# The tail of a convolution–attention–state-space kernel: frequencies in another order, most of the second piece read inside the loop

## The chip, the cores and the metric

The kernel runs on one core of one Trainium2 chip. The metric is device time in microseconds (us) of one execution. A core has a matrix engine (TensorE, PE in the profile, its weight loads PEld), a vector engine (VectorE, DVE), a scalar engine (ScalarE, ACT), GpSimd (POOL) and a sequencer that issues transfers (SyncE, SP). Sixteen DMA engines move data between DRAM and the on-chip memory (SBUF, 128 partitions); transfers are issued here from SP's and from ACT's queue. Each queue issues in order, and an issue that waits holds up everything behind it on its queue.

## The reference, cut to what matters

The input is 8 images of 32 x 32 positions with 128 channels, float32. Layer 0 is a group norm and an attention; layer 1 is a bidirectional state-space block and then a spectral filter bank, and every block adds its input back. The change touches only the end of the last one, which is, for every batch `b`, position `t` and output channel `e`:

```
U_plus  = causal convolution of u with K=16 filters over t          (by FFT)
U_minus = the same of u * (-1)^t, times (-1)^t
out     = einsum('btkd,k,kde->bte', U_plus,  sigma**0.25, M_plus)
        + einsum('btkd,k,kde->bte', U_minus, sigma**0.25, M_minus)
        + sum over i<3 of u[t-i] @ M_u[i]
t       = t + out * keep          # keep: the weight of the bank that a hard softmax picks
```

The kernel does the convolutions with a transform of its own: 128 odd frequencies per block, products with a matrix per frequency, and the transform back.

## The kernel before, in words

**The frequency loop.** The spectra of all batches lie in DRAM (`ud`). A *chunk* is `FC` = 8 of the `NF` = 128 frequencies, so there are 16 chunks. In pass `c` of the loop (`for c in range(-1, chunks)`, L1840) TensorE builds the matrices of chunk `c+1` (`matrices`, L1594, copied out by DVE and ACT at L1605 and L1607) and multiplies the spectra of chunk `c` with the matrices of chunk `c` (`apply`, L1751). A pass has four steps `n`; steps 0 and 1 make the chunk's first four frequencies, steps 2 and 3 its last four. `gather` (L1767 to L1773) adds up the products into `sums`, and `store` (L1779) writes the sums of four frequencies to DRAM, `yd[frequency, block, batch, 2, 4, channel]`, 256 KB. A frequency's row of `yd` has 64 KB: two blocks of 512 positions, each with eight batches; a quarter of it (one block, four batches) is 16 KB and contiguous.

**The pieces.** After the loop the sums are transformed back in four *pieces*, `(k, h)`: block `k`, batches `4h` to `4h+3`. A piece is a tile `yt` of 128 partitions, one frequency in each, 16 KB per partition. For each piece DVE makes `z` (four operations, L1879), TensorE multiplies `inv` with `yt` and `z` for four values of `r` (L1889), DVE multiplies with `keep` and adds the residual, which lies in DRAM as `xa` (L1896), and ACT's queue stores the result (L1899). The last piece is done in two halves of two batches. All of TensorE, DVE, ACT, POOL and SP run in the order in which the program is written (`tc.manual_schedule(engines=ALL_IN_ORDER)`).

**How the pieces get in.** In the order of SP's queue:

- In each pass, the row of the first piece for the eight frequencies of the chunk before is read back from `yd` into `early_yt`, eight rows of 16 KB to eight neighbouring partitions (`fetch`, L1788). SP's transfers of a pass are tied to a product of TensorE (`behind`), which places them within the pass. In the last pass a second fetch reads four more rows, as soon as their store has landed.
- In the last pass the first residual is loaded, 1 MB (`load_residuals`, L1805).
- After the loop the last four frequencies of the first piece are moved from `sums` in SBUF to `early_yt` (`move`, four transfers of 16 KB, L1799), and the last `store` is issued.
- Then come the second piece (`load_piece`, L1864: 112 rows on SP, which need only stores that have long landed, and 16 rows on ACT, which need the last store), its residual, the third piece with its residual and the fourth piece with its residual. A piece is 2.1 MB, a residual 1.05 MB. From the third piece on, the loads read all 128 rows and so wait for the last store.

The pieces 2 to 4 and a residual lie in the room of a chunk's matrices that is no longer needed (`room`).

**The order of the frequencies.** `odd` (L326) holds for each frequency its number 2f+1; the tables of the transform there (`fwd`) and of the filters (`taps`) are made from it, and `alt` (L393) holds the sign (-1)^f. The table of the transform back (`inv`) is made from the partition's number, so partition p of a piece must hold frequency p. Before the change the f-th row of `yd` is frequency f.

Of the kernel before, what the change touches and what calls it, by code (L numbers as in the profile page):

```python
# [14 lines left out]
P = 128  # L15
B = 8
# [16 lines left out]
FC = 8  # L33
PI_1024 = 0.0030679615757712823
# [11 lines left out]
def fast_kernel(ctx: ExitStack, tc: tile.TileContext, a: dict, out: bass.AP, bad: bass.AP):  # L46
# [273 lines left out]
    def transforms(pool, tables):  # L320


        def over_2048(t):
            nc.vector.tensor_scalar(t, t, 1.0 / 2048.0, None, ALU.mult)

        odd = counted(pool, [2, NF], [[512, 2], [2, NF]], 1, 0, "odd")  # L326
        place = counted(pool, [4], [[1, 4]], 0, 4, "place")
        over_2048(place)
        by_place = [(fwd[:, k : k + 1], odd[:, 0:1, :], place[:, k : k + 1]) for k in range(4)]
        turns(by_place[:2])  # L330
        yield
        odd_row = counted(pool, [1], [[1, 1]], 1, 2, "odd_row")
        places = counted(pool, [4, P], [[1, 4], [4, P]], 0, 0, "places")
        over_2048(odd_row)
        yield
        turns(by_place[2:])
        yield
        for _ in angles(pool, fwd, "fwd"):
            yield
        yield  # L340
        turns([(inv, places, odd_row[:, 0:1])])
        for _ in angles(pool, inv, "inv"):
            yield
        yield
        lag = counted(pool, [2, 2], [[-256, 2], [1, 2]], 510, -2, "lag")
        over_2048(lag)
        for h in range(2):
            for r in range(2):
                t = pool.tile([P, 2, 2, NF], F32, name=f"lags{h}_{r}")
                turns([(t, odd, lag[:, h, r : r + 1])])  # L350
                for _ in angles(pool, t, f"lags{h}_{r}"):
                    pass
                tables.append(t)
                yield
        for t in tables:
            sines(t)

    def transform_taps(pool, ps, tables):
# [34 lines left out]
        alt = pool.tile([P, NF // 2, 2], F32, name="alt")  # L393
        nc.gpsimd.memset(alt, 1.0)
        nc.gpsimd.memset(alt[:, :, 1], -1.0)
        alt = alt.rearrange("p f i -> p (f i)")
# [1155 lines left out]
    with ExitStack() as s:  # L1552
# [170 lines left out]
        with ExitStack() as s2:  # L1723
# [60 lines left out]

            def fetch(c, n, rows, other):

                at = slice(c * FC + n * 4, c * FC + n * 4 + rows)
                t = nc.sync.dma_start(  # L1788
                    early_yt[at].rearrange("p b i q e -> p (b i) (q e)"),
                    yd[at, 0, 0:4].rearrange("f b i q e -> f (b i) (q e)"),  # L1790
                )
                behind(t, other)

            def move(c, n, yt, piece):

                at = c * FC + n * 4
                for f in range(4):
                    rows = stored[c, n][f * 32 + piece * 8 : f * 32 + piece * 8 + 8]
                    nc.sync.dma_start(  # L1799
                        yt[at + f : at + f + 1].rearrange("p b i q e -> p (b i) (q e)"),  # L1800
                        rows.rearrange("x q e -> x (q e)"),
                    )

            def load_residuals(k, b, n, other=None):
                t = nc.sync.dma_start(  # L1805
                    res[k][:, b : b + n].rearrange("p b r c -> p b (r c)"),
                    xa[b : b + n, :, k].rearrange("b p r c -> p b (r c)"),
                )
                behind(t, other)

            def amid_products(c, n, made):

                last = c + 1 == chunks
                if n == 0 and c > 0:
                    store(c - 1, 1, made)
                if n == 3 and c > 0:
# [3 lines left out]
                if last and n == 3:  # L1820
                    fetch(c, 0, 4, made)
                if last and n == 0:
                    load_residuals(1, 0, 4, made)
                if not last and n in (1, 2):
# [6 lines left out]
            for c in range(-1, chunks):  # L1831
# [4 lines left out]
                else:  # L1836

                    room = chunk_matrices(c + 1, first_gs)
                    res = [room[:, :32, :], mp.tile([P, 32, C], F32, tag="mst", name="res1")]
                    res = [t.rearrange("p (b r) c -> p b r c", b=B) for t in res]  # L1840
# [13 lines left out]
            pieces = [(k, h) for k in range(NB) for h in range(2)]  # L1854
            yts = [early_yt]
            for n in range(1, 4):
                yts.append(room[:, 32 * n : 32 * n + 32].rearrange("p (b i q) c -> p b i q c", i=2, b=4))
            move(chunks - 1, 1, yts[0], 0)
            store(chunks - 1, 1, None, nc.sync)

            def load_piece(n, rows, engine):

                k, h = pieces[n]
                engine.dma_start(  # L1864
                    yts[n][rows].rearrange("p b i q c -> p (b i) (q c)"),
                    yd[rows, k, h * 4 : h * 4 + 4].rearrange("f b i q e -> f (b i) (q e)"),
                )

            load_piece(1, slice(0, NF - 2 * FC), nc.sync)
            load_piece(1, slice(NF - 2 * FC, NF), nc.scalar)  # L1870
            load_residuals(1, 4, 4)
            for n in range(2, 4):
                load_piece(n, slice(0, NF), nc.sync)
                load_residuals(0, 4 * n - 8, 4)
            for yt, (k, h) in zip(yts, pieces):
# [6 lines left out]
                size = 2 if (k, h) == pieces[-1] else 4  # L1882
                for b in range(0, 4, size):
                    bs = slice(b, b + size)
                    to = res[blk][:, h * 4 + b : h * 4 + b + size]
# [18 lines left out]
                    )  # L1904

# [805 lines left out]
```

## Time and profile before

| | us |
|---|---|
| median of 3 runs | 1382.64 (1382.20 to 1387.87) |
| the profiled execution | 1384.28 |
| its span, first to last instruction | 1382.6 |
| one pass of the loop, 1304.00 to 1320.60 | 16.60 |
| last product of the loop (L1751) ends | 1332.7 |
| first matmul of the pieces 1, 2, 3, 4 (L1889) | 1338.50, 1349.18, 1358.16, 1368.80 |
| stores of the result issued (L1899) | 1348.05, 1357.11, 1367.81, 1374.93, 1376.53 |

All times within the execution are counted from the span's start. Besides the page, which sums up an execution, the trace answers for a stretch how long each engine was busy in it, what granted clock TensorE had, which share of the time the 16 DMA engines were busy and how many GB/s they moved. A timeline lists instructions in order of time: start, duration, engine, line, operation, `written<-read`, count, and in brackets how long the engine had been idle and what ended that. `SPq` and `ACTq` are the issues of transfers; the transfer itself goes on after them. The trace also has each packet that a DMA engine moved, with its size and duration, and the times at which a transfer's semaphore was raised, once by each DMA engine that took part: the last of these is its landing.

### The profile page before, as it was taken

To read this page: it belongs to the slowest core of one execution; us is meant where nothing else is said; L and a number is where in the kernel's file an instruction comes from. 1 tells how busy PE (TensorE), PEld (TensorE's weight loads), DVE (VectorE), ACT (ScalarE), POOL (GpSimd) and SP (SyncE) were. 2 spreads that over 40 slices of the span, in tenths; PEclk is the share of its full clock that TensorE was granted. 3 is DMA by queue.
4 is the path that set the end of the run, shared out by engine and by line. 5 is a ranking of instruction groups with operands and counts; after the bars stand their busy time and mean duration, and the time that the engine had idled before them with its cause. 6 is when DMAs were issued, how large, how long until landed. Compare 5 with 4: busy or idle time off the path is not lost. (4 is left out here: it accounts for less than half of the span.)

```text
span 1382.6 us, 47750 instructions
## 1 busy us (share of the span) xinstructions
PE 1323.1 (96%) x20926; PEld 838.4 (61%) x20926; DVE 1102.9 (80%) x2144; ACT 922.9 (67%) x1429; POOL 551.9 (40%) x606
## 2 busy tenths in 40 slices
PE   7999999999999899999999999998999999999976
PEld 4333333333333566666666666665899999999953
DVE  5789889788868688988898989899775777777744
ACT  5766676766757788888888888787554655555510
POOL 3411986875920333435343434343693211111100
PEclk9999999999999999999999999999999999999999
DMA  7200111111000533434444544441388122222258
GB/s 175 55 2 2 35 44 40 46 48 39 24 9 2 128 87 78 109 78 109 93 94 93 117 94 112 93 110 33 93 275 258 51 78 76 75 77 75 73 156 331
DMA packets 139881, 123.26 MB, mean 89 GB/s; under 512 B 45268, under 2 KB 122708, under 8 KB 135060
## 3 DMA queue, kind: packets, MB, share of 16 engines
q1 hardware_dynamic: 137504, 115.67, 32.3%
q10 hardware_dynamic: 2160, 4.46, 0.9%
q8 instruction: 166, 2.72, 0.8%
q14 instruction: 51, 0.42, 0.1%
HBM read 78.09 MB, written 34.08 MB: 81 GB/s over the span
## 5 line engine op out<-in xcount | busy, mean ns | idle before, releaser
L809 ACT ACTIVATE pr<-pt 128x1024 f32<-128x1024 f32 x256 | 248.1, 1021 | 105.0 <-PE pt L804 104.0
L834 DVE TENSOR_TENSOR two<-pr,pr 128x1024 f32<-128x1024 f32 x128 | 165.0, 1329 | 15.1 <-ACT pr L809 15.1
L1607 ACT COPY gs<-pg 128x512 f32<-128x512 f32 x256 | 132.6, 601 | 60.8 <-PE pg L1594 60.3
L1605 DVE COPY gs<-pg 128x512 f32<-128x512 f32 x256 | 158.9, 684 | 12.7 <-PE pg L1594 9.5
L804 PE MATMUL pt<-q,k 32*128 32x512 f32 x1024 | 162.4, 651 | 6.1 <-ACT pr L809 4.2
L1594 PE MATMUL pg<-taps,mst 32*128 32x128 f32 x4096 | 146.6, 279 | 1.8 <-DVE gs L1605 1.1
L1594 PEld LDWEIGHTS pg<-taps,mst 32*128 32x128 f32 x4096 | 133.2, 186 | 15.2 <-issue 12.1
L825 PE MATMUL po<-pr,v 128*32 128x512 f32 x1024 | 140.6, 610 | 0.0
L1751 PE MATMUL pg<-gs,u 128*32 128x128 f32 (+1 forms) x4096 | 128.5, 277 | 2.4 <-issue 2.4
L1030 POOL TENSOR_TENSOR ec<-ec,ct 128x2048 f32<-128x2048 f32 x16 | 83.7, 5230 | 112.4 <-ACT ct L1110 57.1
L1072 DVE SCALAR_TENSOR_TENSOR xs<-xp,cw,xs 128x1024 f32<-128x1024 f32 x96 | 122.5, 1283 | 2.2 <-issue 0.2
L1582 POOL TENSOR_SCALAR u<-u 128x128 f32<-128x128 f32 x64 | 34.1, 533 | 217.7 <-DMA u<-ud 197.4
L1751 PEld LDWEIGHTS pg<-gs,u 128*32 128x32 f32 (+1 forms) x4096 | 112.2, 141 | 10.1 <-issue 2.6
L1094 PE MATMUL pb<-bxt,wbc 128*128 128x512 f32 x256 | 114.0, 597 | 3.6 <-ACT zs L1085 3.6
L804 PEld LDWEIGHTS pt<-q,k 32*128 32x128 f32 x1024 | 49.6, 186 | 88.9 <-ACT pr L809 27.1
L1302 POOL TENSOR_TENSOR rms<-rms_v,mhalf 128x8 f32<-128x8 f32 x16 | 26.6, 1660 | 157.2 <-DVE rms_v L1300 157.2
L1193 DVE SCALAR_TENSOR_TENSOR state<-state,dec,pst 128x64 f32<-128x64 f32 x448 | 87.3, 275 | 1.1
L1094 PEld LDWEIGHTS pb<-bxt,wbc 128*128 128x128 f32 x256 | 47.1, 189 | 60.4 <-issue 55.0
L825 PEld LDWEIGHTS po<-pr,v 128*32 128x32 f32 x1024 | 27.8, 110 | 89.7 <-issue 86.4
L1016 POOL TENSOR_TENSOR lm<-cs,lm 128x2048 f32<-128x2048 f32 x16 | 57.9, 3622 | 58.0 <-DVE xs L1072 34.7
L845 PE MATMUL pd<-two,ones 128*32 128x512 f32 x512 | 74.2, 618 | 2.4 <-DVE two L834 2.2
L1026 ACT ACTIVATE lm<-lm 128x1024 f32<-128x1024 f32 x64 | 65.7, 1052 | 6.8 <-POOL lm L1016 6.6
(312 smaller groups left out, 2787.7 us busy)
## 6 DMA issues: line engine op xcount, KB each, us to landing
lm<-cd SPq DMA_DIRECT2D x32, 512.0 KB
ec<-cd SPq DMA_DIRECT2D x32, 512.0 KB
ud<-sp SPq DMA_DIRECT2D x8, 1024.0 KB
u<-ud SPq DMA_DIRECT2D x64, 128.0 KB
yd<-sums SPq DMA_DIRECT2D x32, 256.0 KB
moved<-state SPq DMA_DIRECT2D x48, 128.0 KB
X<-in_x SPq DMA_DIRECT2D x8, 512.0 KB
part_p<-in_L_ffn_M_phi_plus SPq DMA_DIRECT2D x32, 128.0 KB
```

What stands on the lines that cost most here:

```text
L804: nc.tensor.matmul(pt[:, i, :], lhsT=k[rows, j * P : (j + 1) * P], rhs=q[rows, cols], start=True, stop=True)
L809: nc.scalar.activation(pr[:, 2 * g : 2 * g + 2, :].rearrange("p i t -> p (i t)"), pt.rearrange("p i t -> p (i t)"), AF.Exp, scale=SCALE,)
L825: nc.tensor.matmul(po[rows, :], lhsT=vs[b][:, j, rows], rhs=pr[:, h, :], start=(j == 0), stop=(j == NT - 1))
L834: nc.vector.tensor_tensor(two, sums["pr"][:, 2 * g : 2 * g + 2, :], pr[:, 2 * g : 2 * g + 2, :], ALU.add)
L1030: t = nc.gpsimd.tensor_tensor(u.ec, u.ec, u.ct.unsqueeze(1).to_broadcast([P, NH, NT, L]), ALU.mult)
L1072: u.convolved = nc.vector.scalar_tensor_tensor(acc, xp[:, at : at + T], cw[u.d][:, n, i : i + 1], acc, ALU.mult, ALU.add)
L1094: nc.tensor.matmul(u.pb[:, i * 512 : (i + 1) * 512], lhsT=wbc[u.d][:, k, :], rhs=xt[:, at : at + 512], start=(k == 0), stop=(k == KC - 1),)
L1193: nc.vector.scalar_tensor_tensor(u.state[:, k, h, :], u.state[:, k - 1, h, :], u.dec[:, c, h, j : j + 1], u.pst[c][:, j, h, :], ALU.mult, ...
L1594: nc.tensor.matmul(pts[g][:, e, :], lhsT=mst[rows, n * 4 + e, :], rhs=taps[rows, cols].rearrange("p f q m i -> p (f q m i)"), start=True, ...
L1605: nc.vector.tensor_copy(to, frm)
L1607: nc.scalar.copy(to, frm)
L1751: product = nc.tensor.matmul(py[t * 32 : t * 32 + 32 - 16 * m, q // 2, :], lhsT=u[:, i, m:, :, :, q * FC + f].rearrange("p k b i -> p (k b ...
```

## The change

1. **Order of frequencies.** Row `j*16+e` of `yd` (e = 0 to 15, j = 0 to 7) now holds frequency `e*8+j`: `odd` and `alt` are made in that order. `inv` is as it was, so that row belongs to partition `e*8+j`. The 16 rows of a pair of chunks `j` go to 16 partitions that lie 8 apart; `places` gives that slice of partitions.
2. **Early rows.** `fetch` and `move` write to those partitions. All four moves are on SP, as before.
3. **First residual.** It has a tile of its own (`first_res`) and is loaded in eight parts of 128 KB, one in each of the passes 2 to 9, behind the first store of the pass.
4. **Second piece.** In the last pass seven pairs (`load_rows`, 16 rows, 256 KB each) are read in the loop: two in step 0, two in step 1, one in step 2, two in step 3, the last two ahead of the four-row fetch. After the loop one pair is left, which holds the last chunks and so waits for the last store. The load on ACT's queue is gone.
5. **Third and fourth piece.** They are still one transfer each on SP, to 128 partitions in order, but the source is read as `(j e) -> e j`: 16 rows 64 KB apart on the outside, 8 steps of 1 MB within.
6. **Residuals.** One tile per piece instead of one per block; the sizes and their places in the order of SP after the loop are as before.
7. **Last piece.** It is done in parts of 2, 1 and 1 batches instead of 2 and 2.

```diff
+FR = 16
...
-        odd = counted(pool, [2, NF], [[512, 2], [2, NF]], 1, 0, "odd")
+        odd = counted(pool, [2, NF // FR, FR], [[512, 2], [2, NF // FR], [2 * NF // FR, FR]], 1, 0, "odd")
+        odd = odd.rearrange("p i j e -> p i (j e)")
...
-        alt = pool.tile([P, NF // 2, 2], F32, name="alt")
+        alt = pool.tile([P, NF // FR // 2, 2, FR], F32, name="alt")
         nc.gpsimd.memset(alt, 1.0)
         nc.gpsimd.memset(alt[:, :, 1], -1.0)
-        alt = alt.rearrange("p f i -> p (f i)")
+        alt = alt.rearrange("p j i e -> p (j i e)")
...
+            def places(row, n):
+
+                j, e = divmod(row, FR)
+                at = e * (NF // FR) + j
+                return slice(at, at + (n - 1) * (NF // FR) + 1, NF // FR)
+
             def fetch(c, n, rows, other):
 
-                at = slice(c * FC + n * 4, c * FC + n * 4 + rows)
+                at = c * FC + n * 4
                 t = nc.sync.dma_start(
-                    early_yt[at].rearrange("p b i q e -> p (b i) (q e)"),
-                    yd[at, 0, 0:4].rearrange("f b i q e -> f (b i) (q e)"),
+                    early_yt[places(at, rows)].rearrange("p b i q e -> p (b i) (q e)"),
+                    yd[at : at + rows, 0, 0:4].rearrange("f b i q e -> f (b i) (q e)"),
                 )
                 behind(t, other)
...
+            pieces = [(k, h) for k in range(NB) for h in range(2)]
+            first_res = yp.tile([P, 4, 4, C], F32, name="first_res")
+            res, yts = [first_res], [early_yt]
...
+            def load_first_residual(part, other):
+
+                b, h = divmod(part, 2)
+                t = nc.sync.dma_start(
+                    first_res[:, b, 2 * h : 2 * h + 2].rearrange("p r c -> p (r c)"),
+                    xa[b, :, NB - 1, 2 * h : 2 * h + 2].rearrange("p r c -> p (r c)"),
+                )
+                behind(t, other)
+
+            def load_rows(n, j, other=None):
+
+                k, h = pieces[n]
+                t = nc.sync.dma_start(
+                    yts[n][places(j * FR, FR)].rearrange("p b i q c -> p (b i) (q c)"),
+                    yd[j * FR : (j + 1) * FR, k, h * 4 : h * 4 + 4].rearrange("f b i q e -> f (b i) (q e)"),
+                )
+                behind(t, other)
+
+            def load_piece(n):
+
+                k, h = pieces[n]
+                nc.sync.dma_start(
+                    yts[n].rearrange("p b i q c -> p (b i) (q c)"),
+                    yd[:, k, h * 4 : h * 4 + 4].rearrange("(j e) b i q c -> e j (b i) (q c)", e=FR),
+                )
 
             def amid_products(c, n, made):
 
                 last = c + 1 == chunks
                 if n == 0 and c > 0:
                     store(c - 1, 1, made)
+                    if 2 <= c < 10:
+                        load_first_residual(c - 2, made)
                 if n == 3 and c > 0:
                     fetch(c - 1, 0, FC, made)
                 if n == (2 if last else 3):
                     store(c, 0, made)
-                if last and n == 3:
-                    fetch(c, 0, 4, made)
-                if last and n == 0:
-                    load_residuals(1, 0, 4, made)
-                if not last and n in (1, 2):
+                if last:
+                    for j in ((0, 1), (2, 3), (4,), (5, 6))[n]:
+                        load_rows(1, j, made)
+                    if n == 3:
+                        fetch(c, 0, 4, made)
+                elif n in (1, 2):
                     for part in (2 * n - 2, 2 * n - 1):
                         load_part(us[c + 1], c + 1, part, made)
...
-            move(chunks - 1, 1, yts[0], 0)
+            move(chunks - 1, 1, 0, nc.sync)
+            move(chunks - 1, 1, 1, nc.sync)
+            move(chunks - 1, 1, 2, nc.sync)
+            move(chunks - 1, 1, 3, nc.sync)
             store(chunks - 1, 1, None, nc.sync)
...
-            load_piece(1, slice(0, NF - 2 * FC), nc.sync)
-            load_piece(1, slice(NF - 2 * FC, NF), nc.scalar)
-            load_residuals(1, 4, 4)
+            load_rows(1, NF // FR - 1)
+            load_residuals(1)
             for n in range(2, 4):
-                load_piece(n, slice(0, NF), nc.sync)
-                load_residuals(0, 4 * n - 8, 4)
+                load_piece(n)
+                load_residuals(n)
...
-                size = 2 if (k, h) == pieces[-1] else 4
-                for b in range(0, 4, size):
+                b = 0
+                for size in (2, 1, 1) if (k, h) == pieces[-1] else (4,):
...
+                    b += size
```

More of the change, by code (lines that the diff above doesn't have):

```diff
@@ L1791, in fetch, with move @@
                 )
                 behind(t, other)
[L1794 to L1804, printed above, removed]
+            def move(c, n, f, engine):
+                rows = stored[c, n][f * 32 : f * 32 + 8]
+                engine.dma_start(
+                    early_yt[places(c * FC + n * 4 + f, 1)].rearrange("p b i q e -> p (b i) (q e)"),
+                    rows.rearrange("x q e -> x (q e)"),
+                )
@@ L1805, in load_residuals @@
+            pieces = [(k, h) for k in range(NB) for h in range(2)]
+            first_res = yp.tile([P, 4, 4, C], F32, name="first_res")
+            res, yts = [first_res], [early_yt]
+            def load_residuals(n, other=None):
+                k, h = pieces[n]
                 t = nc.sync.dma_start(
-                    res[k][:, b : b + n].rearrange("p b r c -> p b (r c)"),
-                    xa[b : b + n, :, k].rearrange("b p r c -> p b (r c)"),
+                    res[n].rearrange("p b r c -> p b (r c)"),
+                    xa[4 * h : 4 * h + 4, :, NB - 1 - k].rearrange("b p r c -> p b (r c)"),
@@ L1811, in amid_products @@
+            def load_piece(n):
+                k, h = pieces[n]
+                nc.sync.dma_start(
+                    yts[n].rearrange("p b i q c -> p (b i) (q c)"),
+                    yd[:, k, h * 4 : h * 4 + 4].rearrange("(j e) b i q c -> e j (b i) (q c)", e=FR),
+                )
             def amid_products(c, n, made):
@@ L1838, in fast_kernel @@
                     room = chunk_matrices(c + 1, first_gs)
-                    res = [room[:, :32, :], mp.tile([P, 32, C], F32, tag="mst", name="res1")]
-                    res = [t.rearrange("p (b r) c -> p b r c", b=B) for t in res]
+                    rest = mp.tile([P, 32, C], F32, tag="mst", name="rest")
+                    for t in (rest[:, :16], room[:, :16], room[:, 16:32]):
+                        res.append(t.rearrange("p (b r) c -> p b r c", b=4))
+                    for n in range(1, 4):
+                        yts.append(room[:, 32 * n : 32 * n + 32].rearrange("p (b i q) c -> p b i q c", i=2, b=4))
                 for n in range(4):
@@ L1852, in fast_kernel @@
                         gather(c, half, turn, py)
[L1854 to L1857, printed above, removed]
-            move(chunks - 1, 1, yts[0], 0)
-            store(chunks - 1, 1, None, nc.sync)
[L1861 to L1867, printed above, removed]
-            load_piece(1, slice(0, NF - 2 * FC), nc.sync)
-            load_piece(1, slice(NF - 2 * FC, NF), nc.scalar)
-            load_residuals(1, 4, 4)
+            move(chunks - 1, 1, 0, nc.sync)
+            move(chunks - 1, 1, 1, nc.sync)
+            move(chunks - 1, 1, 2, nc.sync)
+            move(chunks - 1, 1, 3, nc.sync)
+            store(chunks - 1, 1, None, nc.sync)
+            load_rows(1, NF // FR - 1)
+            load_residuals(1)
             for n in range(2, 4):
-                load_piece(n, slice(0, NF), nc.sync)
-                load_residuals(0, 4 * n - 8, 4)
-            for yt, (k, h) in zip(yts, pieces):
+                load_piece(n)
+                load_residuals(n)
+            for yt, rest, (k, h) in zip(yts, res, pieces):
                 yt = yt.rearrange("p b i q c -> p i b q c")
@@ L1880, in fast_kernel @@
                 blk = NB - 1 - k
-                size = 2 if (k, h) == pieces[-1] else 4
-                for b in range(0, 4, size):
+                b = 0
+                for size in (2, 1, 1) if (k, h) == pieces[-1] else (4,):
                     bs = slice(b, b + size)
-                    to = res[blk][:, h * 4 + b : h * 4 + b + size]
+                    to = rest[:, bs]
                     for r in (0, 2, 1, 3):
```

## The prediction

> **What bounds the kernel now.** I read the page first, then a table of stretches, then the waits and the timeline of the last 50 us.
>
> ```profile
> PE 1323.1 (96%) x20926; PEld 838.4 (61%) x20926; DVE 1102.9 (80%) x2144; ACT 922.9 (67%) x1429; POOL 551.9 (40%) x606
> DMA  7200111111000533434444544441388122222258
> ```
>
> TensorE is busy 96% of the span, and the DMA engines are busy only in the last slices. The stretches (us, busy time by engine in the order PE, PEld, DVE, ACT, POOL, then clock, DMA share, GB/s) separate the loop from the tail:
>
> ```profile
> 1304.00:1320.60 16.60, 16.60 (x519) 15.26 (x516) 12.69 (x29) 9.47 (x22) 3.01 (x8) 1.00 0.29 75
> 1325.00:1330.00 5.00, 4.67 (x170) 4.40 (x162) 1.87 (x8) 0.57 (x3) 0.00 (x0) 1.00 0.95 315
> 1338.40:1347.40 9.00, 8.73 (x16) 3.61 (x16) 4.89 (x8) 0.00 (x0) 0.00 (x0) 0.81 1.00 244
> 1349.10:1356.30 7.20, 7.11 (x16) 2.96 (x16) 4.66 (x7) 0.00 (x0) 0.00 (x0) 1.00 1.03 416
> 1358.10:1367.00 8.90, 8.83 (x16) 3.53 (x16) 4.66 (x7) 0.00 (x0) 0.00 (x0) 0.81 1.03 423
> 1368.80:1376.00 7.20, 7.17 (x32) 6.00 (x32) 5.25 (x11) 0.00 (x0) 0.00 (x0) 1.00 0.65 252
> ```
>
> In a loop pass of 16.60 us TensorE never stops and the DMA engines are 29% busy: transfers there are nearly free. The last pass (second line) is already full, because of the 1 MB residual. The last four lines are the four pieces of the tail: 7.1 us of matmuls each at full clock, 8.7 to 8.8 where the granted clock was 0.5 for part of it. The DMA share is 1.0 throughout, but the first piece's stretch, in which the second piece is loaded, moves only 244 GB/s, against 416 and 423 later. Who waits:
>
> ```profile
> PE pg L1889 <- DMA gs<-yd: 5.6, 3, 2.0
> DVE gs L1896 <- SPq L2681: 4.5, 2, 2.6
> ```
>
> Each later piece comes 1.9 us late to TensorE, and the last two residuals come later still to DVE. The order of issue and the starts:
>
> ```profile
> 1332.03 0.63 PE L1751 MATMUL pg<-gs,u 128*16 128x128 f32 x10 [2.36 <-issue]
> 1333.96 2.75 SPq L1799 DMA_DIRECT2D early_yt<-sums  x4
> 1337.24 0.43 SPq L1864 DMA_DIRECT2D gs<-yd  x1
> 1339.07 0.34 SPq L1864 DMA_DIRECT2D gs<-yd  x1
> 1339.20 0.36 ACTq L1864 DMA_DIRECT2D gs<-yd  x1
> 1349.18 3.67 PE L1889 MATMUL pg<-gs,inv 128*128 128x512 f32 x8 [1.95 <-DMA gs<-yd]
> 1358.16 5.40 PE L1889 MATMUL pg<-gs,inv 128*128 128x512 f32 x8 [1.87 <-DMA gs<-yd]
> 1368.80 1.99 PE L1889 MATMUL pg<-gs,inv 128*128 128x256 f32 x8 [1.81 <-DMA gs<-yd]
> 1373.24 3.25 DVE L1896 SCALAR_TENSOR_TENSOR gs<-pg,keep,gs 128x256 f32<-128x256 f32 x8 [1.89 <-SPq L2681]
> ```
>
> So the tail is one DMA stream that TensorE and DVE follow by 1 to 2 us. DVE ends at 1376.5, the last store lands at 1380.7, the span ends at 1382.6. I work against the profiled run's 1384.28 us; the median of the three is 1382.64, 1.64 less.
>
> **The change, part by part.**
>
> *Tables.* The order of `odd` and `alt` changes, with the same instructions (IOTA 0.34 us at 4.2, while the input loads; MEMSET 0.16 us at 385.2, under matmuls): nothing; without cover under 0.5 us.
>
> *Early rows (L1788).* Same bytes and queue, other partitions; TensorE's full pass hides them: 0.
>
> *First residual.* One 1 MB load in the last pass becomes eight of 128 KB in passes 2 to 9: one more SP issue of 0.4 us behind the pass's first store. Behind it on SP are the next `u` loads, several us later (1189.28 the stores, 1197.36 the loads). Share 0.29 becomes about 0.32: 0.
>
> *Seven pairs (16 rows, 256 KB each) in the last pass.* +1.83 MB, −1.05 MB, in a stretch that is already at share 0.95 for 5 us. On SP seven issues of 0.4 us stand partly ahead of the store and the four-row fetch that waits for it; there the four moves wait for DVE until 1333.96 anyway. TensorE stands 2.36 us on "issue" at 1329.67 in this very stretch, and a 16 KB transfer of the instruction queue started at 1329.59 after none on record since 1322.4, where they come every 4 us: I read it as instructions that came late through full DMA engines. More row loads could lengthen that gap by 3 us, a kinder pattern remove 2.4; I take 0.
>
> *After the loop.* The second piece's 2.1 MB (L1864 on SP and ACT) go; one pair of 256 KB stays and waits for the last store, which landed at 1339.05 (the issue at 1339.07 shows it); behind it on SP stand all the later loads. The stream starts at 1340.2 (1.15 us from issue to first packet, as 1337.24 to 1338.39) instead of 1338.4.
>
> *Third and fourth piece.* Partition e·8+j now takes row j·16+e: the source is 16 steps of 64 KB by 8 steps of 1 MB, no longer 128 equal steps. This decides the case. Three rows bound what it costs. In the third piece now an engine's 16 KB packets last 0.61 us: 8 rows, 4.9 us. In the 112-row load, also cut otherwise, seven packets took 6.5 us per engine, 0.93 each: 7.4 us. And the last fetch, four rows to four neighbouring partitions by four engines, landed 3.6 us after its issue, eight rows to eight neighbours 3.5 us, where a 16 KB move lands in 1.6: four rows to neighbours go one after the other, so neighbouring partitions share one engine's rate. If every engine shares with one other, a row costs 2·0.61 = 1.22 us and a piece 9.8. I take 1.22: sixteen blocks of eight partitions walked in step collide all the way or not at all, and the loads that were cut otherwise all collided.
>
> [...]
>
> Per engine, the stream by these rows: pair 1.2 us, to 1341.4; residual 32 packets of 0.084 us, to 1344.1; third piece 9.8 plus three packets of the first store (which begins at 1351), to 1354.2; residual in turn with the store, 32·0.16 = 5.1, to 1359.3; fourth piece 8·(1.22+0.084) = 10.4, to 1369.7; last residual 24·0.164+8·0.084 = 4.6, to 1374.3. Landing adds 0.4 and the slowest engine 2.1 (1366.65 against 1368.76 now): the fourth piece at 1372.2 (now 1368.76), its residual at 1376.8 (now 1373.15).
>
> *Last piece as 2, 1, 1.* Matmuls over 128 columns repeat every 0.12 us (L601: 44.9 us for 384) against 0.215 over 256: 7.55 us for 7.2. DVE 4·0.41+8·0.25 = 3.6 for 3.25. The last store is 256 KB, 8 packets of 0.084 us fewer: −0.7 (−0.3 to −1.5).
>
> *Clock.* TensorE would stand idle from about 1364 to 1372. After 5.8 us of idling now, the granted clock is 0.5 at first and the piece takes 8.73 instead of 7.11: +1.6.
>
> Sum: matmuls from 1372.2 by 7.55+1.6 to 1381.4, DVE 0.4 more, 1381.8 against 1376.5: +5.3; last store −0.7: **+4.6**. At full clock the residual decides: 1376.8+3.65, so +3.3. 1384.28+4.6 = 1388.9, on the median's scale **1387.2 us**.
>
> **The rivals.**
>
> *R1, faster: the new source costs no bandwidth.* For it: the same bytes, rows and partitions as loads that run at 420 GB/s; against it, every load of `yd` cut otherwise is slow. Third piece to 1349.0, residual 1351.7, fourth 1357.3, its residual 1361.9, landed 1364.4. Then TensorE runs through from 1347.2: 6.9+6.9+7.25 = 1368.3, DVE 1368.7, −7.8, with the store −8.5; a spell of half clock makes it −6.9. I put −8, 1374.6. It decides below about 0.75 us a row.
>
> *R2: the pace of the 112-row load, 0.93 us.* The pieces come 4.7 us sooner than in my sum: about −1, 1381.6.
>
> *R3, slower: the last pass starves.* The row loads, whose packets are eight times as long as the residual's, hold back TensorE's instructions or the store that the four-row fetch waits for on SP, ahead of the moves. For it: the 2.36 us gap. Against: the moves have 1.8 us of room (fetch issued at 1332.14, moves at 1333.96). From 3 us more the last store, and with it the stream, moves by as much: +7.6 to +10, about 1391.
>
> **How the numbers follow.** Mine 0.60 (own range 1384 to 1390.5), R1 0.18, R2 0.10, R3 0.12. 0.5%, about what a measurement of this kernel can tell from no change, is 6.9 us. Faster by more: a little over half of R1, 0.10. Slower by more: 0.07 of mine and most of R3, 0.17. The rest 0.73. The range leaves out most of R1 (0.15) and the end of R3 (0.05): 1378 to 1391.
>
> **What would show it.** Packets of 16 KB in the third and fourth piece at 1.2 us (right), 0.6 (R1) or 0.9 (R2), and under 300 GB/s in those stretches; TensorE into the second piece without a wait, then about 2 us and 8 us of waiting for `gs<-yd`; a half clock at the start of the last piece; the moves still at 1334. The forecast is wrong if the packets stay at 0.6 us, or if the moves slip.

## The result and the profile after

The changed kernel takes 1389.72 us at the median, the kernel before 1384.64 us in the same comparison (18 runs of each): a ratio of 1.004, 95% interval 1.0023 to 1.0058, or 3 to 8 us slower. The forecast was 1387.2 from 1382.64, a ratio of 1.0033. The profiled execution took 1392.09 us, with a span of 1390.3.

From the page of the changed kernel, TensorE's totals and the DMA share in 40 slices:

```profile
PE 1326.3 (95%) x20942; PEld 842.4 (61%) x20942; DVE 1104.0 (79%) x2148; ACT 922.3 (66%) x1429; POOL 551.1 (40%) x606
DMA  7200111111000533444444544431387233222378
```

TensorE's share fell from 96 to 95%: it works 3 us longer than before (1326.3 for 1323.1) in a span that is 7.7 us longer, so most of the rest is waiting. The DMA engines, at 5 and 8 tenths in the last two slices before, now stand at 7 and 8. Their stretches in the end (us, busy time of PE, PEld, DVE, ACT, POOL, then clock, DMA share, GB/s): the last pass, and TensorE's four pieces.

```profile
1326.90:1335.82 8.92, 6.84 (x236) 6.30 (x228) 3.52 (x16) 1.06 (x4) 0.00 (x0) 1.00 0.94 251
1342.50:1351.40 8.90, 8.89 (x14) 3.85 (x15) 4.51 (x7) 0.00 (x0) 0.00 (x0) 0.67 0.83 230
1352.40:1359.45 7.05, 7.03 (x17) 2.85 (x15) 5.22 (x8) 0.00 (x0) 0.00 (x0) 1.00 0.99 207
1360.20:1367.40 7.20, 7.13 (x16) 2.96 (x16) 4.54 (x9) 0.00 (x0) 0.00 (x0) 1.00 1.10 352
1374.70:1384.25 9.55, 9.46 (x48) 8.19 (x48) 6.47 (x16) 0.00 (x0) 0.00 (x0) 0.77 0.91 349
```

The third line is the reading that matters: while TensorE does the second piece and the third is being loaded, the engines are busy all the time (0.99) and move 207 GB/s. In the answering line of before (1349.10 to 1356.30, shown with the prediction) they moved 416 at 1.03. In a window that holds almost nothing but the third piece's load, the DMA view of the changed kernel has this for SP's queue (packets, MB, share of 16 engines):

```profile
q1 hardware_dynamic: 111, 1.82, 104.7%
```

The window is 1349.7 to 1358.0: 1.047 · 16 · 8.3 us over 111 packets of 16 KB are 1.25 us a packet. The kernel before has, for 1351.0 to 1354.5 of its third piece:

```profile
q1 hardware_dynamic: 82, 1.34, 90.4%
```

That is 0.904 · 16 · 3.5 us over 82 packets of 16 KB, 0.62 us each on average (median 0.61). The order of issue, DVE's last sums and the starts of TensorE, from the timeline of the changed kernel:

```profile
1333.92 0.63 PE L1753 MATMUL pg<-gs,u 128*16 128x128 f32 x10 [0.81 <-issue]
1335.53 0.28 DVE L1775 TENSOR_TENSOR sums<-both 128x128 f32<-128x128 f32 x1
1337.05 0.62 SPq L1796 DMA_DIRECT2D early_yt<-yd  x1
1337.77 2.78 SPq L1805 DMA_DIRECT2D early_yt<-sums  x4
1342.51 6.62 PE L1922 MATMUL pg<-early_yt,inv 128*128 128x512 f32 x8 [7.96 <-DMA early_yt<-sums]
1342.72 0.54 SPq L1835 DMA_DIRECT2D gs<-yd  x1
1352.40 3.60 PE L1922 MATMUL pg<-gs,inv 128*128 128x512 f32 x8
1360.21 3.70 PE L1922 MATMUL pg<-gs,inv 128*128 128x512 f32 x8 [0.78 <-DMA gs<-yd]
1374.71 3.78 PE L1922 MATMUL pg<-gs,inv 128*128 128x256 f32 x8 [7.36 <-SPq L2715]
```

TensorE goes into the second piece (1352.40) without a wait, as the change provides, waits 0.78 us for the third and 7.36 us for the fourth (the profile puts the latter down to SP; the DMA records have the fourth piece landing at 1374.67). Ahead of the first piece two things are new: the gap of 2.36 us in the last pass is down to 0.81, and the four moves go out 1.96 us after DVE's last sums were ready (1335.81), where before it was 0.03 us.

**Where the time went.** I set the traces side by side at the last addition of the pass before the last one (`both<-pg,half`), the first line from the kernel before, the second from the changed one:

```profile
1323.00 0.29 DVE L1768 TENSOR_TENSOR both<-pg,half 128x128 f32<-128x128 f32 x1 [0.88 <-ACT half L1767]
1326.77 0.29 DVE L1770 TENSOR_TENSOR both<-pg,half 128x128 f32<-128x128 f32 x1 [0.85 <-ACT half L1769]
```

From there to the end of the span it is 59.6 us before and 63.5 after: +3.9. The other 3.8 us of the two spans' difference arose earlier. The fourteen passes before that point took 232.7 us before and 234.8 after; two kernels below that have before's loop unaltered took 232.6 and 234.9, so 2 us there is a difference between executions and no effect of the change that these traces could show. The other 1.7 us lie ahead of those passes.

On this common clock (the changed kernel's times less 3.77 us) DVE's last sums are ready 1.9 us earlier than before (1332.04 for 1333.93), but the moves go out at the same time (1334.00 for 1333.96), and so does the last store (1336.82 for 1336.75): the changed kernel's last pass gained time, and the wait on SP took it away again.

### The profile page after: what moved, and what is told of

Read it like the earlier page. It is cut to its first block, busy times and chain, and to the rows that moved or that the text cites. A ratio compares the mean times of both kernels' runs of the same rounds, so it can differ in the third digit from the quotient of the medians.

```text
span 1390.3 us, 47791 instructions
## 1 busy us (share of the span) xinstructions
PE 1326.3 (95%) x20942; PEld 842.4 (61%) x20942; DVE 1104.0 (79%) x2148; ACT 922.3 (66%) x1429; POOL 551.1 (40%) x606
```

## The experiments

Two theories were tested. *Form*: the new form of the load halves its rate, and that alone makes the kernel slower; the earlier load of the second piece is a gain. *Last pass*: the last pass starves (the first piece is late because of waits on SP and of what the pass reads), and that is the loss. All ratios are to the kernel before, run beside each on the same chip.

### One part alone: the source of 16 by 8 rows

```
     def load_piece(n, rows, engine):          # kernel before
+        if n > 1: src = yd[:, k, ...].rearrange("(j e) b i q c -> e j (b i) (q c)", e=16)
```

> The kernel before with one edit: the third and fourth piece are read with the changed kernel's source pattern, 16 rows outside by 8 rows within. The frequencies of these two pieces then stand on wrong partitions, so that half of the spectral filter's output is not the reference's; the work is the same. Theory A (the cut of such a source over the DMA engines makes pairs of them share one way into SBUF): 16 KB packets of these pieces last 1.2 us instead of 0.61, each piece comes about 5 us later than the one before it, and the end is 8 to 10 us later, ratio about 1.006 to 1.007. Theory B (the form of the load is harmless, and the changed kernel lost its time to the fuller last pass and the later start of the stream): packets 0.6 us, within 1.5 us of the kernel before.

Measured: 1392.28 us, ratio 1.0061 (1.0039 to 1.0084). Its timeline:

```profile
1346.26 3.67 PE L1890 MATMUL pg<-gs,inv 128*128 128x512 f32 x8 [0.94 <-DMA gs<-yd]
1359.55 6.06 PE L1890 MATMUL pg<-gs,inv 128*128 128x512 f32 x8 [6.19 <-DMA gs<-yd]
1374.34 3.78 PE L1890 MATMUL pg<-gs,inv 128*128 128x256 f32 x8 [5.30 <-DMA gs<-yd]
```

The waits ahead of the third and fourth piece, 1.87 and 1.81 us before, are 6.19 and 5.30: 7.8 us more, for a time that rose by 8.4 (0.0061 of 1384). The 16 KB packets took 1.13 us in the third piece (1350 to 1358). By the medians the load form alone costs more than the whole change does; the two intervals overlap, so that the rest of the change gains something has to be shown by the repaired kernel below.

### The same form with near rows

In words, in place of the source:

```
+        src = rows 7*e + j of yd, e = 0..15, j = 0..7     # steps of 448 KB and 64 KB
```

> As the kernel with the 16 by 8 source, but the 16 outer rows are 7 rows (448 KB) apart and the 8 inner ones neighbours (64 KB), in place of 64 KB and 1 MB; rows are read twice or not at all, so the output of two pieces is wrong. Theory A (the cut over engines and partitions): packets still last 1.2 us and the end is 8 to 10 us later than before. Theory C (the steps of 1 MB in DRAM are what is slow): packets are back at 0.6 us, end within 1.5 us of before.

Measured in one execution: 1395.89 us; waits of 6.60 and 5.68 us ahead of the third and fourth piece, 16 KB packets of 1.10 us between 1352 and 1358.

```profile
1363.28 6.36 PE L1892 MATMUL pg<-gs,inv 128*128 128x512 f32 x8 [6.60 <-DMA gs<-yd]
1378.75 3.74 PE L1892 MATMUL pg<-gs,inv 128*128 128x256 f32 x8 [5.68 <-DMA gs<-yd]
```

There is no step of 1 MB any more in this load, and it is as slow. The steps of 1 MB in DRAM are not the cause.

### The whole change with its load form repaired

The rows are put into `yd` in the order of the partitions when they are stored, so that a piece is again read in 128 equal steps.

```
-    yd[at : at + 4].rearrange("f k b i q e -> (f k b i) (q e)")       # store
+    yd[places(at, 4)].rearrange("f k b i q e -> f (k b i) (q e)")     # last chunk: four stores, a row each
-    yd[:, k, ...].rearrange("(j e) b i q c -> e j (b i) (q c)", e=FR) # load_piece
+    yd[:, k, ...].rearrange("f b i q c -> f (b i) (q c)")
```

> The changed kernel with its order of frequencies, pairs and parts, but the stores put each row where its partition's number says, so that the third and fourth piece are read as 128 equal steps again (the pairs and the early rows are read in steps of 8 rows). Each store in the loop has four separate rows; the two of the last chunk are four transfers each. Theory A: packets of both pieces 0.61 us, 400 GB/s or more while they run, TensorE waits for at most one of them, end 7 to 11 us earlier than the changed kernel, that is 2 to 6 us (0.15 to 0.45%) under the kernel before. Theory B: still 4 to 6 us above the kernel before.

Measured: 1380.83 us, ratio 0.9979 (0.9965 to 0.9992); by the medians' ratios that is 0.6%, 8.4 us, below the changed kernel, about what the form cost when it was put in alone. The timeline of the repaired kernel:

```profile
1329.72 0.63 PE L1753 MATMUL pg<-gs,u 128*16 128x128 f32 x10 [0.56 <-issue]
1341.84 5.36 PE L1930 MATMUL pg<-early_yt,inv 128*128 128x512 f32 x8 [11.49 <-DMA yd<-sums]
1366.24 1.99 PE L1930 MATMUL pg<-gs,inv 128*128 128x256 f32 x8 [1.88 <-DMA gs<-yd]
```

Between the first and the fourth piece TensorE now waits for no load, for the fourth 1.88 us, and the packets take 0.62 us (1347.0 to 1349.5). But the first piece starts 11.49 us after the last product, against 5.84 before and 7.96 in the changed kernel. So the load's form is settled as the loss. In this kernel the late first piece eats up what the early load gains; 3.5 us of that come with the repair itself, whose last chunk has eight stores on SP instead of two.

### Moves in place of the four-row fetch, in two kernels

In the changed kernel the four-row fetch waits for a store (landed 1336.99, the fetch went out at 1337.05) and stands ahead of the last moves. Here it goes, and the rows of the chunk's first half come out of `sums` in SBUF like the last ones.

```
-                    if n == 3: fetch(c, 0, 4, made)
+                    if c + 1 == chunks and n == 2:
+                        for f in range(4): move(c, 0, f, nc.sync)
```

First on top of the repaired kernel:

> As the one with the scattered store, and the four-row fetch of the last pass, which waits on SP for the store of the same rows, is replaced by four moves from SBUF. If that wait holds back the last moves (in the changed kernel they were issued 1.9 us after DVE had their data), the moves come within 0.3 us of DVE's last sum, the first piece 1.5 to 2 us earlier, and the end 1 to 2 us earlier than with the scattered store alone: 3 to 8 us under the kernel before. If TensorE or the stream is bound elsewhere: no difference between the two.

Measured: 1384.32 us, ratio 0.9989 (0.9969 to 1.0009), not faster than the repaired kernel. Its timeline and its waits on SP:

```profile
1328.71 5.65 SPq L1813 DMA_DIRECT2D early_yt<-sums  x4
1339.05 2.76 SPq L1813 DMA_DIRECT2D early_yt<-sums  x4
1344.73 6.45 PE L1931 MATMUL pg<-early_yt,inv 128*128 128x512 f32 x8 [13.39 <-DMA yd<-sums]
```

```profile
SPq L1813 <- DMA yd<-sums: 2.9, 1, 2.9
```

The last of the first four moves waited 2.9 us for a store whose data it does not need. That store is the eighth issue back on SP. In the trace of the changed kernel SP's issues from 1300.92 to 1345.32 raise eight semaphores in turn (100 to 106 and 108), so each shares one with the eighth issue back; I read the move's wait as one for this semaphore. More transfers in the last pass made a new wait.

Then on the changed kernel itself:

> The changed kernel, with the four-row fetch of chunk 15's first half (which waited for the store of those sums, landed 1336.99, and stood ahead of the last moves) replaced by four moves out of the sums in SBUF, issued in the third step of the last pass; same result. Theory 'slip': the last moves go out when DVE's last sums are ready (about 1335.9 instead of 1337.77 on the changed kernel's clock), the first piece, the store of the last sums, the pair's load behind it and so the whole stream come about 1.9 us earlier: 1.5 to 2.5 us faster than the changed kernel, ratio to the kernel before 1.002 to 1.003 (changed kernel 1.004), gaps ahead of the third and fourth piece as in the changed kernel (0.8 and 7.4 us). Theory 'only the rate counts': another wait of SP takes the fetch's place, nothing gained, ratio 1.0035 to 1.0045.

Measured: 1391.99 us, ratio 1.0044 (1.0028 to 1.0059). Against the changed kernel's 1.004 nothing was gained.

```profile
1337.34 0.63 PE L1753 MATMUL pg<-gs,u 128*16 128x128 f32 x10 [1.73 <-issue]
1339.88 2.74 SPq L1805 DMA_DIRECT2D early_yt<-sums  x4
1345.43 6.27 PE L1923 MATMUL pg<-early_yt,inv 128*128 128x512 f32 x8 [7.46 <-DMA early_yt<-sums]
1376.13 3.78 PE L1923 MATMUL pg<-gs,inv 128*128 128x256 f32 x8 [7.26 <-DMA gs<-yd]
```

The moves now go out 0.65 us after DVE's last sums (1339.23) instead of 1.96. TensorE nevertheless starts 6.2 us after the sums, against 6.7 with the fetch and 4.6 before: two pair loads had been issued just ahead of the moves (1338.66 and 1339.19), and the last move landed 3.1 us after its issue (1341.99 to 1345.08), where the answering one of before took 2.2. With the fetch gone, the row loads hold the moves up themselves. And the wait ahead of the fourth piece is as long as ever (7.26), so the end stays where the stream puts it. This does not rule the 'slip' out: counted from the last addition of the pass before, the moves went out only 0.2 us earlier than in the changed kernel, and the interval still holds 1.003.

### The first residual alone

```
-                if last and n == 0: load_residuals(1, 0, 4, made)        # kernel before
+                if n == 0 and 2 <= c < 10: load_first_residual(c - 2, made)
```

> The kernel before, with one part of the change alone: the first piece's residual is read in eight parts in passes 2 to 9 instead of in one MB in the last pass; same result. Theory 'bytes beside the last pass hold TensorE up': the 2.36 us issue gap ahead of the last ten matmuls shrinks to under 1 us as in the changed kernel (0.81), and all behind it comes earlier: 1.5 to 2.5 us faster than before, ratio 0.998 to 0.999. Theory 'chance': the gap is a matter of the run and not of that load; the time stays within 0.1% of before, ratio 0.9995 to 1.0005. If the eight small loads cost the loop something, ratio over 1.0005.

Measured: 1383.95 us, ratio 0.9985 (0.9972 to 0.9999).

```profile
1332.78 0.63 PE L1751 MATMUL pg<-gs,u 128*16 128x128 f32 x10 [0.30 <-issue]
```

With no large load in the last pass the gap is 0.30 us instead of 2.36. Three more kernels that keep before's last pass, the two with the altered source above and the one with neighbouring partitions below, have it at 1.50, 1.40 and 1.55. So the gap comes with that load, though its length varies from one execution to the next.

### The early load without a new order of rows

Before's order and load forms, the first residual in passes 2 to 9, 112 consecutive rows of the second piece in one load at the start of the last pass, the moves instead of the fetch.

```
+                if last and n == 0: load_piece(1, slice(0, NF - 2 * FC), nc.sync, made)
-            load_piece(1, slice(0, NF - 2 * FC), nc.sync)                # after the loop
-            load_piece(1, slice(NF - 2 * FC, NF), nc.scalar)
+            load_piece(1, slice(NF - 2 * FC, NF), nc.sync)
```

> The kernel before with the early part of the change alone and no new order of rows: the first residual in passes 2 to 9, 112 consecutive rows of the second piece in one load at the start of the last pass, its last 16 rows after the last store, four moves instead of the four-row fetch; third and fourth piece are loaded as before, in 128 equal steps; same result. Theory 'the early part is good and the load form spoils it': the 1.95, 1.87 and 1.81 us that TensorE waited for the second, third and fourth piece go (5.6 us), the packets of the third and fourth piece stay at 0.61 us, the last piece no longer meets half a clock: ratio 0.995 to 0.997, 1377 to 1379 by before's 1383. Theory 'the last pass has no room': the store of chunk 15's first half and the last moves stand behind the load's 7 packets an engine (8 us), or TensorE's instructions come late; the first piece starts 3 us or more after 1338.5, ratio 0.998 to 1.001.

Measured: 1379.57 us, ratio 0.9952 (0.9934 to 0.997).

```profile
1338.47 0.63 PE L1751 MATMUL pg<-gs,u 128*16 128x128 f32 x10 [3.34 <-issue]
1345.82 6.15 PE L1903 MATMUL pg<-early_yt,inv 128*128 128x512 f32 x8 [6.71 <-DMA early_yt<-sums]
```

After 1345.82 no wait of TensorE over 0.25 us is left; the three of before are gone. The last pass pays: 3.34 us on "issue".

### Half of that load

```
-                    load_piece(1, slice(0, NF - 2 * FC), nc.sync, made)
+                    load_piece(1, slice(0, NF // 2), nc.sync, made)
-            load_piece(1, slice(NF - 2 * FC, NF), nc.sync)
+            load_piece(1, slice(NF // 2, NF), nc.sync)
```

> The kernel of the early load without a new order of rows, with 64 rows of the second piece instead of 112 in the last pass and the other 64 after the last store; same result. Theory 'bytes beside the last pass hold TensorE up' (issue gap in the last pass 3.34 us with 112 rows and 2.36 us with the 1 MB residual, 0.30 us with no load there): a load of half the length, over some 4 us earlier, leaves a gap under 1 us, the last moves stand behind nothing, the first piece starts 2 to 4 us earlier against the end of the pass before (17.5 us there, before 15.5), and the other 64 rows (4 to 5 us), the residual and the third piece still land before TensorE needs them: ratio 0.993 to 0.9945. Theory 'the gap is chance, and the rows left to the stream cost a wait': a wait of 1 us or more ahead of the second or third piece, ratio 0.995 to 0.998.

Measured: 1386.13 us, ratio 1.0009 (0.9995 to 1.0023), slower than both theories said; the wait that the second one named did come (1.43 us, ahead of the third piece).

```profile
1335.12 1.04 PE L1751 MATMUL pg<-gs,u 128*16 128x128 f32 x10 [5.15 <-issue]
1359.39 3.70 PE L1903 MATMUL pg<-gs,inv 128*128 128x512 f32 x8 [1.43 <-DMA gs<-yd]
1370.03 3.56 PE L1903 MATMUL pg<-gs,inv 128*128 128x256 f32 x8 [3.51 <-DMA gs<-yd]
```

Half the bytes made the longest gap of all, and the rows left to the stream cost 1.43 and 3.51 us. The idea that the gap grows with the load's length was wrong. What the DMA records do show is when the instruction queue's 16 KB transfer ran. In eight kernels the gap ends 1.3 to 1.7 us after that transfer does:

| kernel | transfer starts | ends | TensorE goes on | gap |
| --- | --- | --- | --- | --- |
| before | 1329.59 | 1330.63 | 1332.03 | 2.36 |
| changed | 1331.05 | 1332.39 | 1333.92 | 0.81 |
| first residual early | 1329.91 | 1331.30 | 1332.78 | 0.30 |
| 112 rows in one load | 1335.78 | 1336.90 | 1338.47 | 3.34 |
| 64 rows in one load | 1332.03 | 1333.79 | 1335.12 | 5.15 |
| moves for the fetch | 1334.34 | 1335.69 | 1337.34 | 1.73 |
| repaired form | 1326.88 | 1328.01 | 1329.72 | 0.56 |
| every seventh row (below) | 1325.34 | 1326.59 | 1328.07 | 1.23 |

In the five kernels left out of the table it ends 1.3 to 1.4 us after the transfer. The gap is thus read as the wait for this transfer, and it is roughly as long as the transfer is late: 0.30 us where it starts 3.9 us after the 16 KB transfer before it, 2.36 at 7.2 us, 3.34 at 8.1 and 5.15 at 8.6. That it is late because it waits behind row packets on its DMA engine is argued: the records do not name the engine. Why 64 rows delayed it more than 112 is open; the 16 KB packets in the stretch of the 64-row load took 1.20 us on average (1324 to 1336), those in the stretch of the 112-row load 0.99 (1327 to 1338), and when the transfer becomes due against the load may matter too.

### The third and fourth piece as row loads

```
-                load_piece(n)                                            # changed kernel
+                for j in range(NF // FR): load_rows(n, j)
```

> The changed kernel, with the third and fourth piece read as eight loads of sixteen rows each (one row an engine, into every eighth partition) instead of one load with a source of 16 by 8 rows; same result. Theory 'which partitions are written at one time' : sixteen rows a step of eight partitions apart collide as the one load's did (the pair loads of the last pass took 1.1 to 1.25 us a packet too): packets 1.1 to 1.25 us, 9 to 10 us a piece, ratio to before 1.002 to 1.006 as the changed kernel. Theory 'the 16 by 8 form of one load': packets 0.61 to 0.7 us, 5 to 6 us a piece, the wait ahead of the fourth piece (7.36 us) goes, ratio 0.995 to 0.999.

Measured: 1393.99 us, ratio 1.0051 (1.0033 to 1.007); packets of 1.22 us between 1346 and 1354, waits of 7.23 and 3.24 us.

```profile
1332.43 0.64 PE L1753 MATMUL pg<-gs,u 128*16 128x128 f32 x10 [1.41 <-issue]
1363.49 6.19 PE L1923 MATMUL pg<-gs,inv 128*128 128x512 f32 x8 [7.23 <-DMA gs<-yd]
1376.35 3.75 PE L1923 MATMUL pg<-gs,inv 128*128 128x256 f32 x8 [3.24 <-DMA gs<-yd]
```

So the form of one transfer is not what is slow. What this kernel and, by the prediction's argument, the changed one share is the set of partitions that is written at one time, sixteen, eight apart; that any load of one row an engine might be slow is what the next two kernels test.

### Sixteen neighbouring partitions

```
-                load_piece(n, slice(0, NF), nc.sync)                     # kernel before
+                for j in range(NF // 16): load_piece(n, slice(16 * j, 16 * j + 16), nc.sync)
```

> The kernel before, with the third and fourth piece each read as eight loads of sixteen consecutive rows into sixteen consecutive partitions (one row an engine), rows and partitions in their old places; same result. Theory 'partitions that lie in one group share a way in': sixteen partitions eight apart took 1.2 us a packet of 16 KB, sixteen neighbours share fewer ways, so the packets take 2 us or more, a piece 16 to 20 us, and the time rises by 15 to 25 us (1400 to 1408). Theory 'any load of one row an engine runs at half rate': packets 1.1 to 1.25 us, about 10 us a piece, 1391 to 1395.

Measured in one execution: 1407.81 us, and in the trace:

```profile
1370.08 5.47 PE L1890 MATMUL pg<-gs,inv 128*128 128x512 f32 x8 [15.91 <-DMA gs<-yd]
1390.71 3.66 PE L1890 MATMUL pg<-gs,inv 128*128 128x256 f32 x8 [11.73 <-SPq L2682]
```

The packets take 2.15 us in the fourth piece (1377 to 1385); in the third, beside the first store's small packets, they took 1.46 on average (1349 to 1363). These loads and the row loads above read the same rows in DRAM sixteen at a time, in the same packets: 1.22 or 2.15 us a packet by the partitions alone. The 0.61 us of 128 equal steps is a load of another form.

That neighbours share fewer ways in was the theory's assumption. The runs show the packet times alone; the records name no engine and no partition of a packet.

### Every seventh row

Sixteen rows to a load as in the changed kernel, but into every seventh partition, with before's order of rows, and two to three loads a step.

```
-                if last and n == 0: load_piece(1, slice(0, NF - 2 * FC), nc.sync, made)
+                if last:
+                    for j in ((0, 1), (2, 3, 4), (5, 6), ())[n]:
+                        load_piece(1, slice(j, NF - 2 * FC, 7), nc.sync, made)
```

> The kernel of the early load without a new order of rows (112 rows in one load, ratio 0.9952), with those 112 rows read as seven loads of sixteen rows, every seventh row into every seventh partition, two in the first step of the last pass, three in the second, two in the third; same result. Theory 'an instruction fetch of TensorE waits behind the packets queued on its DMA engine' (16 KB fetch at 1329.59, 1335.78 and 1332.03 in three kernels, the gap over 1.4 to 1.6 us after its end): with two or three packets queued on an engine instead of seven, the gap in the last pass is 0.3 to 1.7 us instead of 3.34, the pass lasts 8.2 to 9.3 us instead of 11.15, and the third and fourth piece keep their 0.61 us packets and find TensorE busy: 2 to 3 us faster than with one load, ratio 0.993 to 0.9945. Theory 'what the last pass reads comes out again behind it': the last moves stand behind the late loads and the first piece starts as late as with one load, ratio 0.995 to 0.997.

Measured: 1377.80 us, ratio 0.9941 (0.9921 to 0.9961), the fastest kernel here.

```profile
1328.07 0.63 PE L1751 MATMUL pg<-gs,u 128*16 128x128 f32 x10 [1.23 <-issue]
1338.06 5.85 PE L1904 MATMUL pg<-early_yt,inv 128*128 128x512 f32 x8 [9.35 <-DMA early_yt<-sums]
```

The row packets of the last pass take 0.91 us (1322 to 1328), those of the changed kernel's last pass 1.08 (1330 to 1336). Why they take 0.91 and not 0.61 is left open. The gap is in the range expected, the pass lasts 9.47 us, just above it (11.15 with one load), and behind the first piece no wait of TensorE over 0.25 us follows. The rival was half right too: the first piece starts 8.1 us after DVE's last sums (1329.97), 3.5 us later than before, because two row loads stand just ahead of the moves (1329.01 and 1330.12), which go out at 1331.26. Its interval overlaps with that of the one load, so which of the two is faster is not settled; both beat the kernel before, and the changed kernel.

Of all kernels, these carry the verdict (tail: from the last `both` of the pass before the last to the end of the span, in the profiled execution):

| kernel | ratio | gap in last pass | tail |
| --- | --- | --- | --- |
| before | 1 | 2.36 | 59.6 |
| changed | 1.004 | 0.81 | 63.5 |
| load form alone | 1.0061 | 1.50 | 68.4 |
| changed, form repaired | 0.9979 | 0.56 | 58.7 |
| first residual alone | 0.9985 | 0.30 | 58.9 |
| early load, before's form, one load | 0.9952 | 3.34 | 55.8 |
| early load, every seventh row | 0.9941 | 1.23 | 54.9 |

The load form is the loss, and the early load is a gain. The waits of TensorE and of SP in the last pass cost part of that gain.

## Why the prediction was right, and where it was not

**Third and fourth piece: right.** 1.22 us a packet was forecast; the third piece took 1.25, the fourth 1.06. Putting this part in alone made the kernel 0.6% slower, taking it out of the change made it 0.6% faster. R1 (the form costs nothing) and R2 (0.93 us) fall. Steps of 1 MB in DRAM are not the cause either: 1.10 us a packet without any (near rows). The reason given was that engines share a rate by the partitions they write: that the partitions decide is shown by the row loads eight apart (the same 1.22 us) and by neighbours (2.15). That it is just one other engine was an estimate, 2·0.61 us; it fits the 1.22, but no run shows it, as the records name neither engines nor ways in. One row it was read from says less than it was made to say: the four packets of before's last fetch did not go one after the other, they ran side by side (1333.01 to 1334.32, 1.04 to 1.24 us each), and only their landings were late (1335.83 to 1335.98).

**The first residual and the seven pairs: the 0 held, as the sum of two things.** They were taken at 0, with −2.4 to +3 as bounds. The gap shrank by 1.55 us in the profiled execution and DVE's last sums came 1.9 us earlier on the common clock, but the moves did not. How much of the shorter gap is the change's doing is not settled: the kernel with row loads for the third and fourth piece, whose last pass is the same, has a gap of 1.41 us, and its sums came only 0.2 us earlier; before's last pass has gaps of 1.40 to 2.36 in four executions. The residual alone is worth 0.15% (0.01 to 0.28%), about 2 us. That the gap is late instructions fits all thirteen kernels, in which it ends 1.3 to 1.7 us after the instruction queue's transfer.

**"The moves still at 1334": right in time, not in the reason.** On the common clock the moves went out at 1334.00, the pair's load at 1338.95 (1339.07 was forecast) and its first packet at 1340.3 (1340.2). The prediction had the moves wait for DVE; they waited for the four-row fetch, 1.96 us beyond DVE's sums. This is R3's mechanism, for which the prediction allowed 0.12: the store that the fetch needs took 5.8 us to land (1331.20 to 1336.99) for 4.4 before, with row packets on the engines. The 1.8 us of room that the prediction gave the fetch were just used up. In the kernel with row loads for the pieces the same wait put the moves 0.9 us later than before. So R3's wait is there, but R3's price, which begins at 3 us of delay, was not reached.

**The fourth piece: right.** Forecast to land at 1372.2, its residual at 1376.8. On the common clock they landed at 1370.9 and 1375.9. The 1.3 us are the fourth piece's eight packets an engine, 1.06 us each instead of 1.22.

**The wait ahead of the third piece: too long.** 2 us forecast, 0.78 measured. TensorE itself was later: the first piece took 9.9 us (1342.51 to 1352.40) for 8.7 before, with a granted clock of 0.67 over that stretch, behind 7.96 us of idling, for 0.81 behind 5.84 us before. The 8 us ahead of the fourth piece were 7.36.

**The last piece: right.** 9.15 us of matmuls forecast with the half clock, 9.46 measured; the clock is 0.77 over that stretch. From DVE's end to the end of the span it is 5.70 us (1384.56 to 1390.26) for 6.06: −0.36, inside −0.3 to −1.5 and half of the −0.7 taken.

**Tables, early rows, loads in the passes: 0.** Nothing in the traces speaks against it, but the loop varies by 2 us between executions, so less than that is not shown.

The sum, +4.6, stands against +5.5 (3.2 to 8.0) in the comparison and +3.9 in the tail of the profiled execution. The 0.7 us between sum and tail are the fourth piece's earlier landing (−1.3), the longer matmuls (+0.3) and the smaller gain of the last store (+0.35). The main term, the rate of the two loads, was right in its size, by the packets; the sharing it was put down to fits and is not shown. That the stream started to 0.1 us when it was forecast to was luck in part: DVE's earlier sums and SP's wait for the fetch, neither of them in the sum, cancelled in this execution; in the kernel with row loads the pair's load was 0.75 us later than forecast.

## What to carry to other kernels

Before a load is given a new order, ask which partitions the sixteen DMA engines write at the same moment: the packet size, the byte count and the DMA share can all stay as they were while, as here, the rate halves (1.22 us a packet for 0.61) or falls to less than a third (2.15). If an order of rows is wanted, put it into the store, and count the issues that this adds (eight stores instead of two made the first piece 3.5 us later here), or into loads whose packets turn out shorter (in the last pass 0.91 us with every seventh partition, 1.08 with every eighth), and leave the big loads as 128 equal steps. A transfer moved under a busy engine was not free here even where all its data came in time (with rows of the second piece read in the last pass TensorE stopped there for 0.56 to 5.15 us, and the changed kernel's moves went out 1.96 us late): look at the instruction queue's transfers and at what stands on SP ahead of the next small move.

## What was not expected of the hardware

- One 16 KB row packet took 1.22 or 2.15 us with equal bytes and sources, by the partitions that the loads write, eight apart or neighbours, and 0.61 in a load of 128 equal steps.
- TensorE stopped for 0.3 to 5.15 us at the end of the loop, each time until 1.3 to 1.7 us after a 16 KB transfer of the instruction queue. Half a load (64 rows) gave a longer stop than a whole one (112 rows).
- A small move waited 2.9 us for a store eight issues earlier, of which it needed nothing.
